# The order of ScalarE's work in slot 0 of a Mamba scan loop

## Chip, cores and metric

One core of one Trainium2 chip runs the whole kernel in float32. The metric is the device time of one launch in microseconds, the median of several runs. One core has five engines with separate instruction queues: TensorE (PE), VectorE (DVE), ScalarE (ACT), GpSimd (POOL) and SyncE (SP), which here issues the DMAs. In the profile PEld is TensorE's loading of weights.

## What is computed

The input x has 16 images of 96 channels and 64 x 64 pixels. Layer 0 is a graph convolution: a 1x1 convolution, then in each 8 x 8 window the 9 nearest of 64 nodes, an edge product with GELU, the maximum over the neighbours, another 1x1 convolution and a residual. Layer 1 runs two Mamba blocks over the 4096 pixels as a sequence, then a fusing 1x1 convolution, batch normalisation and a residual. The part of the reference that the change concerns:

```python
mu = seq.mean(-1, keepdims=True)
var = ((seq - mu) ** 2).mean(-1, keepdims=True)
h = (seq - mu) * jax.lax.rsqrt(var + EPS) * ln_g + ln_b
xz = h @ in_w
...
delta = jax.nn.softplus(dt @ dt_w + dt_b)
A = -jnp.exp(A_log)
dA = jnp.exp(delta[..., None] * A)
dBx = delta[..., None] * Bm[:, :, None, :] * xc[..., None]
...
hstates = jax.lax.associative_scan(comb, (dA, dBx), axis=1)[1]
y = jnp.einsum('blds,bls->bld', hstates, Cm) + Dp * xc
y = y * jax.nn.silu(z)
return y @ out_w
```

Here the model width is 96, the inner width 192, and there are 16 states.

## The kernel before

The sequence of each image is cut into 8 pieces of 512 pixels. An *item* is one piece in one of the two Mamba blocks of one image; there are 256 items, numbered n = 16 b + 8 i + k (image b, block i, piece k). The 16 states of an item are taken in pairs, so that an item has 8 *slots*, p = 0 to 7, and the main loop (L742 on) runs over 2048 slots. In a slot VectorE does three products `db` of `u` with `bt` (L646) and three scans (L788); ScalarE makes the three decays `da` that the scans read (L635); TensorE spreads one pair of rows of B over the partitions into `bt` (L641), one slot ahead; GpSimd multiplies the scanned states with C (L804); TensorE adds these up over the states (`folded`, L654 to L659), one slot behind. When the last fold of an item is done, in slot 0 of the next one, `gate` multiplies the sum with the gate z (L665, L666) in slot 1. VectorE, the product before the gate and the scans after it stand in one queue.

The instructions of each engine run in the order in which the program issues them. That order is written by hand: the rest of the work is held in Python generators, each of which issues one step per slot, after the slot's first scan. They stand in two lists:

- `preps`: the preparation of the item two ahead (`prelude`). It starts in slot 4. Its fifth step falls into slot 0 of the next item and is the softplus: Exp, +1, Ln, -1 on ScalarE (L595, L597, L599, L600). GpSimd takes it up in slot 1 (L602).
- `going`: `norm` of the item two ahead, whose first step in slot 0 is the product `pc` (L521) and its Square on ScalarE (L523), and whose second in slot 1 is `pvar` (L526), Ln and Exp (L528, L529); `tail`, which for an item of the second block has in slot 0 the fusing product `po` (L690) and its copy `o` on ScalarE (L692); `edges` and `nearest`, the graph convolution of later pieces. In slot 0 `edges` has the products `pv` (L386, L387) and their copy `vu` on ScalarE (L389). In slot 2 and 3 it has the products `t` and the GELUs (L406 to L414).

The products of these steps share a pool of two PSUM tiles, `pm`, tag "mm", in rotation: a product waits until the reader of the last but one is done. `bt` has one PSUM tile of its own.

The decays and the C rows (`ct`) of a slot are issued by `ahead`, two slots before they are used (`AHEAD = 2`). As a rule that is done at the end of a slot, unless a step in the slot has changed ScalarE's table of functions (it yields `TABLE`). In the slots of `FIRST` it is done ahead of the slot's steps. The lines in the slot:

```python
                open_steps()
                if p in FIRST:
                    ahead()
                held = False
                for several in (preps, going) if p == 0 else (going, preps):
                    for steps in list(several):
                        step = next(steps, several)
```

Of the kernel before, what the change touches and what calls it, by code (L numbers as in the profile page):

```python
# [20 lines left out]
def tile_conv_knn_mamba(ctx: ExitStack, tc: tile.TileContext, w: dict, out: bass.AP):  # L21
# [248 lines left out]
    def close_steps():  # L270
        while closing:
            products, use = closing.pop(0)
            opening.append(partial(use, products()))

    def open_steps():
        while opening:
            opening.pop(0)()
# [205 lines left out]
    def pooled(b):  # L483

        mean = pr.tile([C, 1], F32, tag="mean1", name=f"mean1_{b}")
        nc.vector.reduce_sum(mean, means.pop(b), AX.X)
        yield
        pg = pm.tile([C, 1], F32, tag="mm", name=f"pg_{b}")
        nc.tensor.matmul(pg, lhsT=gpT, rhs=mean, start=True, stop=True)
        yield  # L490
        gp = pr.tile([C, 1], F32, tag="gp", name=f"gp_{b}")
        nc.scalar.activation(gp, pg, AF.Relu, bias=gp_b[:, 0, :], scale=1.0 / L)
        yield
        gc = pr.tile([C, 1], F32, tag="gc", name=f"gc_{b}")

        def product():
            ps = pm.tile([C, 1], F32, tag="mm", name=f"pg2_{b}")
            nc.tensor.matmul(ps, lhsT=fusT[:, 1, :], rhs=gp, start=True, stop=True)
            return ps

        apart(product, lambda ps: nc.vector.tensor_tensor(gc, ps, fus_b[:, 0, :], ALU.add))
        yield
        gcs[b] = gc
# [6 lines left out]
    def norm(n):  # L510

        b, i, k = items[n]
        nm = f"{b}_{i}_{k}"
        seq = seqs[b, k]
        hn = hns[n % NHN]
        if k == 0:
            nc.gpsimd.memset(hn[:, :HALO], 0.0)
        else:
            nc.gpsimd.tensor_copy(hn[:, :HALO], hns[(n - 1) % NHN][:, Q:])
        pc = pm.tile([C, Q], F32, tag="mm", name=f"pc_{nm}")  # L520
        nc.tensor.matmul(pc, lhsT=cmat, rhs=seq, start=True, stop=True)  # L521
        sq = pr.tile([C, Q], F32, tag="sq", name=f"sqv_{nm}")
        nc.scalar.activation(sq, pc, AF.Square)  # L523
        yield
        ps = pm.tile([C, Q], F32, tag="mm", name=f"pvar_{nm}")
        nc.tensor.matmul(ps, lhsT=ones_cc, rhs=sq, start=True, stop=True)  # L526
        rs = pr.tile([C, Q], F32, tag="rs", name=f"rs_{nm}")
        nc.scalar.activation(rs, ps, AF.Ln, bias=eps_t[:C], scale=1.0 / C)  # L528
        nc.scalar.activation(rs, rs, AF.Exp, scale=-0.5)  # L529
        yield  # L530
        nc.gpsimd.tensor_tensor(hn[:C, HALO:], seq, rs, ALU.mult)  # L531
# [107 lines left out]
    def bcast(n, p):  # L639
        bt = pb.tile([128, Q], F32, tag="bt", name=f"bt_{n}_{p}")  # L640
        nc.tensor.matmul(bt, lhsT=bsel[:, p, :], rhs=made[n][2], start=True, stop=True)  # L641
        return bt

    def times_b(n, p, c, bt):
        db = pd.tile([128, Q], F32, tag="db", name=f"db_{n}_{p}_{c}")
        nc.vector.tensor_tensor(db, made[n][5][:, c, :], bt, ALU.mult)  # L646
        return db
# [15 lines left out]
    def gate(n, y):  # L663
        z = made[n][1]
        nc.vector.tensor_tensor(z[:, :Q], z[:, :Q], y[0], ALU.mult)  # L665
        nc.vector.tensor_tensor(z[:, Q:], z[:, Q:], y[1], ALU.mult)  # L666

    def tail(n):

        b, i, k = items[n]  # L670
        nm = f"{b}_{i}_{k}"
        seq = seqs[b, k]
        z = made[n][1]

        def product():
            po = pm.tile([C, Q], F32, tag="mm", name=f"pow_{nm}")
            nc.tensor.matmul(po, lhsT=out_w[i][:, 0, :], rhs=z[:, :Q], start=True, stop=False)
            for h in range(2):
                nc.tensor.matmul(
                    po[:, bass.ts(h, QH)], lhsT=out_w[i][:, 1 + h, :], rhs=z[:, Q:], start=False, stop=(h == 1)  # L680
                )
            return po

        apart(product, lambda po: nc.vector.tensor_tensor(seq, seq, po, ALU.add))  # L684
        del made[n]
        if i == NL - 1:
            yield
            yield
            po = pm.tile([C, Q], F32, tag="mm", name=f"po_{nm}")
            nc.tensor.matmul(po, lhsT=fusT[:, 0, :], rhs=seq, start=True, stop=True)  # L690
            o = pr.tile([C, Q], F32, tag="xn", name=f"o_{nm}", bufs=1)
            nc.scalar.activation(o, po, AF.Identity, bias=gcs[b])  # L692
            yield
            yield
            nc.vector.bn_stats(stats[:, b * NQ + k, :], o)
            nc.sync.dma_start(out=o_d[b][:, bass.ts(k, Q)], in_=o)
# [21 lines left out]
        drain(prelude(n))  # L718

    AHEAD = 2  # L720
    FIRST = (0, 2, 4)
    order = [(n, p) for n in range(NI) for p in range(NPR)]
    coming = deque(order)
    soon = {}
# [1 line left out]
    def ahead():  # L726
        if coming:
            t = coming.popleft()
            soon[t] = chosen(*t)
# [5 lines left out]
    going, preps = [edges(0, NQ - 2)], []  # L735
# [6 lines left out]
    for m, (n, p) in enumerate(order):  # L742
        b, i, k = items[n]
        nm = f"{b}_{i}_{k}"
        after = order[m + 1] if m + 1 < len(order) else None

        if n % 2 == 1 and p == 5 and near_row < NB * NQ:
            going.append(nearest(*divmod(near_row, NQ)))
            near_row += 1
        if n % 2 == 1 and p == 5 and edge_row < NB * NQ:  # L750
            going.append(edges(*divmod(edge_row, NQ)))
            edge_row += 1
        between.extend(later[0])
        later = [later[1], []]
        if p == 0 and k == 0:
            state = pr.tile([128, NPR, NB3], F32, tag="state", name=f"state_{nm}")
        if p == 0 and i == 0 and k == 5:
            going.append(pooled(b))
        if p == 0 and n + 2 < NI:
            going.insert(0, norm(n + 2))  # L760
        if p == 4 and n + 2 < NI:
            preps.append(prelude(n + 2))
        ct, das = soon.pop((n, p))
        dbs = [first, times_b(n, p, 1, bt), times_b(n, p, 2, bt)]
        if after is not None:
            bt = bcast(*after)
        hb = pr.tile([128, NB3, Q], F32, tag="hb", name=f"hb_{nm}_{p}", bufs=3)
        for c in range(NB3):
            if c == 1:
                if p == 1 and n:  # L770
                    gate(n - 1, y)
                if p == 6 and n:
                    going.append(tail(n - 1))
                open_steps()
                if p in FIRST:
                    ahead()
                held = False

                for several in (preps, going) if p == 0 else (going, preps):
                    for steps in list(several):  # L780
                        step = next(steps, several)
                        held = held or step is TABLE
                        if step is several:
                            several.remove(steps)
                close_steps()
            if c == 2 and after is not None:
                first = times_b(*after, 0, bt)
            nc.vector.tensor_tensor_scan(  # L788
                hb[:, c, :], das[c], dbs[c], state[:, p, c : c + 1] if k else 0.0, ALU.mult, ALU.add
            )  # L790
            if between and c < 2 and p not in (0, 1):
                between.popleft()()  # L792
            while c == 1 and late:
                late.pop(0)()
        if behind is not None:
            if p == 1:
                y = [
                    py.tile([128, Q], F32, tag="ya", name=f"ya_{nm}"),
                    py.tile([128, QH], F32, tag="yb", name=f"yb_{nm}"),
                ]  # L800
            folded(*behind, y)
        if k + 1 < NQ:
            nc.gpsimd.tensor_copy(state[:, p, :].unsqueeze(2), hb[:, :, Q - 1 : Q])  # L803
        nc.gpsimd.tensor_tensor(hb, hb, ct.unsqueeze(1).to_broadcast([128, NB3, Q]), ALU.mult)  # L804
        behind = (n, p, hb)
        while not held and len(soon) < AHEAD and coming:
            ahead()
# [53 lines left out]
```

## Time and profile before

| | |
|---|---|
| median of 3 runs | 13931.91 us (13919.25 to 13937.55) |
| the profiled execution: its time | 13931.85 us |
| the profiled execution: its span | 13930.0 us |
| mean granted TensorE clock | 0.953 of full speed |
| first scan starts | 401.86 us into the span |

A page of the profile lists for each group of instructions their line, engine, operation, tiles, count, busy time and mean length, then the idle time of the engine before them and what ended it. The scans and products dominate VectorE: 6144 products `db` of 685 ns and 6144 scans, most of them of 1276 ns. A wait is read as "engine, tile, line, waiting for engine, tile, line". Idle time of an engine matters only if it is the one that sets the end, or if it hands its lateness on to that one.

### The profile page before, as it was taken

Reading aid. Unit: us, or ns where it says so; the run is one execution under the profiler, and the core shown is the slowest. Engines: PE = TensorE matmul, PEld = TensorE weight load, DVE = VectorE, ACT = ScalarE, POOL = GpSimd, SP = SyncE. Lnnn points to the kernel's source line nnn. Section 1 sums busy time; section 2 is a strip of 40 time slices with the busy share of each in tenths; the row PEclk is TensorE's granted clock in tenths of the full one; section 3 lists DMA queues with packets and bytes.
Section 4 is the critical chain, followed back from the end, with each engine's and each line's share of the span. In section 5 each row is a group of like instructions: output and inputs, shape, how many; then the busy total and the mean of one; then the engine's idle time right before and its main releaser. Section 6 shows DMA issues by size and latency. Waiting matters only on the chain. (4 is left out here: it accounts for less than half of the span.)

```text
span 13930.0 us, 162083 instructions
## 1 busy us (share of the span) xinstructions
PE 12335.4 (89%) x47944; PEld 4659.8 (33%) x47944; DVE 12860.6 (92%) x16894; ACT 9963.9 (72%) x14645; POOL 10740.5 (77%) x6407
## 2 busy tenths in 40 slices
PE   5899999999999999999999999999999999999881
PEld 2333333333333333333333333333333333333320
DVE  2799999999999999999999999999999999999994
ACT  4677777777777777777777777777777777777652
POOL 1687878788787787878788787887878888787781
PEclk8999999999999999999999999999999999999995
DMA  1233333333333333333333333333333333333327
GB/s 27 74 83 88 87 80 88 85 82 87 85 84 86 85 85 83 85 84 83 87 85 84 85 87 82 84 87 84 84 87 86 81 87 86 81 85 88 81 81 230
DMA packets 887144, 1206.19 MB, mean 87 GB/s; under 512 B 282272, under 2 KB 413742, under 8 KB 877040
## 3 DMA queue, kind: packets, MB, share of 16 engines
q1 hardware_dynamic: 871792, 1169.34, 32.4%
q10 hardware_dynamic: 14464, 26.48, 0.5%
q8 instruction: 377, 6.18, 0.2%
q14 instruction: 511, 4.19, 0.1%
HBM read 706.82 MB, written 85.72 MB: 57 GB/s over the span
## 5 line engine op out<-in xcount | busy, mean ns | idle before, releaser
L804 POOL TENSOR_TENSOR hb<-hb,ct 128x1536 f32<-128x1536 f32 x2048 | 7067.0, 3451 | 599.9 <-issue 190.9
L788 DVE TENSOR_TENSOR_SCAN hb<-da,state,db 128x512 f32<-128x512 f32 x5376 | 6842.8, 1276 | 0.0
L646 DVE TENSOR_TENSOR db<-u,bt 128x512 f32<-128x512 f32 x6144 | 4009.7, 685 | 201.5 <-PE bt L641 198.4
L635 ACT ACTIVATE da<-delta,a 128x512 f32<-128x512 f32 x6144 | 3904.8, 716 | 30.1 <-DVE hb L788 19.4
L641 PE MATMUL bt<-dbl,bsel 128*128 128x512 f32 x4096 | 2359.8, 659 | 279.0 <-DVE db L646 269.5
L657 PE MATMUL ya<-hb,fold 128*64 128x512 f32 x8192 | 2273.9, 634 | 123.9 <-POOL hb L804 123.2
L803 POOL COPY state<-hb 128x3 f32<-128x3 f32 x1792 | 335.9, 187 | 1942.0 <-DVE hb L788 1846.2
L414 ACT ACTIVATE g<-t,eb,es 128x512 f32<-128x512 f32 x1536 | 1171.8, 776 | 899.2 <-PE t L406 655.3
L659 PE MATMUL yb<-hb,fold 128*64 128x256 f32 x8192 | 1284.4, 393 | 0.0
L659 PEld LDWEIGHTS yb<-hb,fold 128*64 128x64 f32 x8192 | 610.5, 142 | 1252.6 <-issue 1251.7
L641 PEld LDWEIGHTS bt<-dbl,bsel 128*128 128x128 f32 x4096 | 627.0, 193 | 1143.7 <-DVE db L646 632.3
L406 PE MATMUL t<-oh,vu 128*128 128x512 f32 x2048 | 985.6, 603 | 20.8 <-ACT g L414 20.8
L788 DVE TENSOR_TENSOR_SCAN hb<-da,db 128x512 f32<-128x512 f32 x768 | 926.6, 1213 | 16.1 <-ACT da L635 16.1
L548 PE MATMUL pj<-hn,conv_in 128*128 128x512 f32 x2048 | 929.2, 596 | 9.1 <-POOL hn L531 9.1
L560 ACT ACTIVATE xc<-pj,conv_b 128x512 f32<-128x512 f32 (+1 forms) x512 | 297.1, 580 | 797.8 <-PE pj L553 671.8
L657 PEld LDWEIGHTS ya<-hb,fold 128*64 128x64 f32 x8192 | 498.8, 140 | 1038.1 <-issue 610.2
L375 POOL TENSOR_SCALAR oh<-idb,node 64x1024 f32<-64x1024 uint16 x256 | 730.8, 2855 | 126.3 <-DMA idb<-idxd 126.3
L409 PE MATMUL t<-oh,vu 128*64 128x512 f32 x2048 | 553.3, 618 | 183.5 <-ACT g L414 180.4
L528 ACT ACTIVATE rs<-pvar,eps_t 96x512 f32<-96x512 f32 x256 | 174.7, 683 | 689.8 <-PE pvar L526 687.7
L792 DVE TENSOR_REDUCE hqa<-g 128x64 f32<-128x512 f32 x976 | 651.3, 667 | 0.0
L406 PEld LDWEIGHTS t<-oh,vu 128*128 128x128 f32 x2048 | 390.2, 193 | 528.8 <-issue 413.7
L548 PEld LDWEIGHTS pj<-hn,conv_in 128*128 128x128 f32 x2048 | 392.6, 192 | 510.5 <-issue 498.1
(166 smaller groups left out, 17319.8 us busy)
## 6 DMA issues: line engine op xcount, KB each, us to landing
ct<-cd SPq DMA_DIRECT2D x4096, 128.0 KB
delta<-ln SPq DMA_DIRECT2D x1024, 128.0 KB
u<-s SPq DMA_DIRECT2D x1024, 128.0 KB
idb<-idxd SPq DMA_DIRECT2D x256, 256.0 KB
delta<-ln SPq DMA_DIRECT2D x1024, 64.0 KB
u<-s SPq DMA_DIRECT2D x1024, 64.0 KB
x<-in_x SPq DMA_DIRECT2D x128, 192.0 KB
rn<-r4d SPq DMA_DIRECT2D x128, 192.0 KB
```

The lines of the kernel that those rows point to most:

```text
L375: nc.gpsimd.tensor_scalar(ohj, numbers, node, None, ALU.is_equal)
L406: nc.tensor.matmul(t, lhsT=vus[p][:, part, :128], rhs=ohw[part], start=True, stop=True)
L414: nc.scalar.activation(g, t, AF.Gelu, bias=e_b[:, j : j + 1], scale=e_s[:, j : j + 1])
L548: nc.tensor.matmul(ps, lhsT=wt[:, t, :128], rhs=hn[:, off : off + Q], start=(t == 0), stop=(t == taps - 1))
L635: nc.scalar.activation(da, delta[:, c, :], AF.Exp, scale=a_neg[i][:, c, p : p + 1])
L641: nc.tensor.matmul(bt, lhsT=bsel[:, p, :], rhs=made[n][2], start=True, stop=True)
L646: nc.vector.tensor_tensor(db, made[n][5][:, c, :], bt, ALU.mult)
L657: nc.tensor.matmul(y[0][half(h)], lhsT=fold, rhs=hb[:, h, :], start=False, stop=(p == NPR - 1))
L659: nc.tensor.matmul(y[1][half(h)], lhsT=fold, rhs=hb[:, 2, bass.ts(h, QH)], start=False, stop=(p == NPR - 1))
L788: nc.vector.tensor_tensor_scan(hb[:, c, :], das[c], dbs[c], state[:, p, c : c + 1] if k else 0.0, ALU.mult, ALU.add)
L792: between.popleft()()
L804: nc.gpsimd.tensor_tensor(hb, hb, ct.unsqueeze(1).to_broadcast([128, NB3, Q]), ALU.mult)
```

## The change

Two edits, both in the main loop:

```diff
     AHEAD = 2
-    FIRST = (0, 2, 4)
+    FIRST = (2, 4)
...
                 held = False
-
-                for several in (preps, going) if p == 0 else (going, preps):
+                for several in (going, preps):
```

With the first, the decays and C rows of slot 2, which slot 0 issued before its steps, are issued at its end, as in slots 1, 3, 5, 6 and 7. With the second, the softplus in slot 0 is issued after the steps of `going` and not before them. In slot 0 ScalarE has then: the Square, `vu`, `o` where there is one, the four softplus passes, the three decays. Before it had: the three decays, the four softplus passes, the Square, `vu`, `o`. No instruction is added or removed.

## The prediction

> **What bounds the kernel now.** First the page's busy times (engine, busy us, share of the span, instructions):
>
> ```profile
> PE 12335.4 (89%) x47944; PEld 4659.8 (33%) x47944; DVE 12860.6 (92%) x16894; ACT 9963.9 (72%) x14645; POOL 10740.5 (77%) x6407
> ```
>
> VectorE is the bound; it stands still for 1069 us of the 13930.0 us span. About half of that lies before the first slot, in the first two items or in the closing normalisation, which the change doesn't touch. So next the waits of DVE alone (total us, times, longest us):
>
> ```profile
> DVE z L665 <- PE ya L657: 359.9, 121, 5.0
> DVE db L646 <- PE bt L641: 198.4, 202, 48.0
> ```
>
> The gate of the previous item (L665) waits for its last fold on TensorE in 121 of 256 items. That is the largest stall inside the loop. Some 57 us of the second row fall at the start; about 140 us are short waits in slots 2 and 3. Why the fold is late is read from the timeline of one item (start us, length us, instruction, count, idle before it and its releaser):
>
> ```profile
> 7010.36 3.79 ACT L635 ACTIVATE da<-delta,a 128x512 f32<-128x512 f32 x6
> ...
> 7011.68 1.02 PE L521 MATMUL pc<-x,cmat 96*96 96x512 f32 x2
> ...
> 7017.55 0.57 ACT L523 ACTIVATE sqv<-pc 96x512 f32<-96x512 f32 x1
> ...
> 7018.18 2.02 PE L690 MATMUL po<-x,fusT 96*96 96x512 f32 x2 [4.67 <-ACT sqv L523]
> ...
> 7022.15 0.69 DVE L665 TENSOR_TENSOR z<-z,ya 128x512 f32<-128x512 f32 x1 [4.54 <-PE ya L657]
> ```
>
> The reader is to see the chain: pc is ready at 7012.70, but its square starts at 7017.55, since ScalarE has six decays and four softplus passes (7014.03 to 7017.65) ahead of it. The product L690 needs the PSUM buffer that the square frees, so it waits 4.67 us, and the fold (7020.13, behind it on PE) lets the gate go only at 7022.15. The fold's operand was ready at 7013.87, when L804 ended.
>
> Two more lines of the same kind name what gets worse. Who waits for the logarithm L528 (total us, times):
>
> ```profile
>   PEld pv L386: 94.2, 120
> ```
>
> 120 is the number of even items with edges: there slot 1 takes one PSUM tile more (L308), so pv comes back to the buffer that L528 reads. In item 148, even and without L690, this reads:
>
> ```profile
> 8111.88 0.68 ACT L528 ACTIVATE rs<-pvar,eps_t 96x512 f32<-96x512 f32 x1 [2.00 <-PE pvar L526]
> ...
> 8116.35 1.13 PE L641 MATMUL bt<-dbl,bsel 128*128 128x512 f32 x2
> ...
> 8118.31 0.67 DVE L646 TENSOR_TENSOR db<-u,bt 128x512 f32<-128x512 f32 x1
> ```
>
> bt ends at 8117.48 and DVE wants it at 8118.31: 0.83 us of slack between L528 and a DVE stall.
>
> **What the Trainium skill says.** *PSUM — Partial Sum Buffer*, section "Engine vs sequencer instructions": ScalarE's queue is strictly first in, first out, and matmuls start and complete in program order. The chain above is just that: one waiting square holds ScalarE's work behind it, one waiting product holds the fold. *TensorE: Matmul & The Clock Gate*, "What's actually happening": the array falls to half rate after an idle window of about 3.4 us, and the windows run free. The trace agrees: L690 takes 2.02 us above and 1.10 us in item 138, where PE waited less; and a less idle PE is cut too, in item 153:
>
> ```profile
> 8357.60:8361.10 3.50, 1.27 (x3) 0.44 (x4) 3.47 (x9) 3.35 (x6) 3.40 (x2) 1.00 0.17 60
> 8361.10:8364.50 3.40, 3.40 (x11) 1.13 (x12) 3.40 (x5) 1.55 (x4) 2.31 (x4) 0.50 0.24 77
> ```
>
> (stretch; its length and PE's busy us; PEld, DVE, ACT, POOL; granted clock, DMA.) With 1.27 us of 3.50 busy the next stretch gets clock 0.50. *ScalarE: Activation LUTs*, "What ACT_TABLE_LOAD costs": a load takes about 1283 ns and consecutive ACTIVATEs overlap by about 93 ns. The trace shows 1283 ns, and the loads stand at L414, L451, L560 and L567 only, in slots 2 to 5; the moved instructions already run side by side without one, so the change adds none.
>
> **The change part by part.** Nothing is added or removed; in slot 0 ScalarE's order goes from [da for slot 2 x3, softplus x4, square, vu, (o)] to [square, vu, (o), softplus x4, da x3]. PE's and POOL's order stays: neither moved step issues there. On SP the two ct loads of slot 2 go behind the slot's other DMAs (in even items the x1 store, which waits for L475); their reader, L804 of slot 2, comes some 15 us later, so this costs nothing. The decays are wanted at slot 2's first scan.
>
> I walk ScalarE through slot 0 with the trace's durations: three decays 1.98, softplus 3.62, square 0.57, vu 0.46, o 0.68, and sort the items by parity and by whether L690 stands in slot 0 (n mod 16 in 10 to 15, 0, 1; about 60 of each kind that matter).
>
> *Odd with L690* (the item above): decays of slot 1 end at 7012.34; square 7012.74 to 7013.31; vu to 7014.0; L690 follows pv directly, 7013.5 to 7014.6 at full rate; fold to 7016.2. DVE comes to the gate at 7017.6: no wait. o ends at 7015.4, softplus at 7018.9, the decays at 7020.8, before a second slot that starts at about 7023. Length of slot 1 from first scan to first scan: 11.60 us now, 6.69 in odd items without L690. Gain 60 x 4.9 = 294 us.
>
> *Odd without L690*: no gate wait now. But the square is late here too; pvar (L526) waits 1.4 us for it, PE's idle time adds up and the clock halves (item 153), and bt comes 2.26 us late. With the square early that idle time goes. Waits in slots 2 and 3 of n mod 16 = 3, 7, 9: 12.6 + 7.1 + 21.7 = 41 us; lost overlap 2; and I take 10 of the 21 us in items 5, where pooling adds its own wait. Gain 53 us.
>
> *Even without L690* (item 148): pc ends only at 8106.70, behind pf2, fold and bt on PE, while ScalarE has done slot 1's decays by 8103.7. It used to fill those 3 us with the decays and softplus that now stand behind. Square to 8107.31, vu 8107.54 to 8108.00, softplus to 8111.53, decays to 8113.41, L528 at 8113.32 instead of 8111.88: 1.44 later. pv and bt follow it on PE: bt ready at 8118.95, wanted at 8118.31: 0.65 us stall in slot 2. The table load and gelus of slot 2 are 1.44 late too; next bt ready 8124.8, wanted 8123.61 + 0.65: 0.53. By slot 4 there was 1.6 us of slack, so it ends there. With 0.08 of lost overlap per wait, 1.34 us, 61 items: loss 82 us. Bounds: 0 (if PE finds room) to 2.7 (if its clock halves as well).
>
> *Even with L690*: now 2.24 us of waits per item in some four pieces, 2.6 with the overlap. The gate's wait goes, but o also stands ahead of softplus: in item 138 L528 comes at 7586.1, bt at 7591.8 against a wish at 7590.4: 1.36, then 0.45. PE is idle 2.6 us before pv, so the clock will mostly halve, about 1.2 more. After: 2.9; loss 0.3 x 60, say 20 us; bounds -1 to +1.5 per item.
>
> Sum: -294 - 53 + 82 + 20 = -245. From the profiled execution's own 13931.85 us (the median of the runs is 13931.91, the same) this gives about 13687 us.
>
> **Rivals.**
> 1. *As worked out*, the stall of odd items goes and even items pay a little: 13687, own range 13630 to 13760. Chance 0.58.
> 2. *Even items don't pay*: L528's lateness is absorbed. -294 - 53 and up to -100 from the even items with L690: 13931.85 - 347 - 50 = 13535, or up to 13585 with little from those. For: POOL and DVE have no other wait there. Against: pv's 120 waits on L528 show that this edge is already live. 0.12.
> 3. *Even items pay double*, PE idle before pv halving the clock in both kinds: 61 x 2.7 = 165 and 60 x 1 = 60; 13931.85 - 347 + 225 = 13810. 0.19.
> 4. *The fold stays late* for another reason, say o or POOL's L804, so the stall keeps its size: 13930. Against: L804 is done at 7013.87. 0.04.
> 5. *Slower*: pv behind L528 becomes the new gate wait. ScalarE idles in slot 0 of even items until pc, everything behind slides, L528 comes 3 or more us late instead of 1.44, PE idles, runs at half clock, and bt is late in slots 2, 3 and 4. It decides from 347/121 = 2.9 us more per even item; at 4 us the time is 13931.85 - 347 + 484 = 14069. For: both halves of the mechanism are in the trace. Against: ScalarE's walk leaves 2 us less than that. 0.07.
>
> Differences under 0.2% (28 us) can't be told from no change here. Faster: 1, 2, 3 and a little of the rest, 0.89; same 0.04; slower 0.07. The range that holds 8 in 10 takes case 1, most of 3 and the near end of 2: 13580 to 13830.
>
> **What would show it.** Right: L665's wait on L657 falls below 40 us; L690 no longer waits for L523 and takes near 1.1 us; slot 1 of odd items is 6.7 us in all. The even items' cost: pv's wait on L528 grows from 94 to some 250 us and DVE's wait for bt stays near 200 us though the odd items' part is gone. Wrong: DVE waiting for da (L635) in slot 2, which would mean that the decays are late; waits for bt above 400 us, which would mean case 5; L665 still waiting, case 4.

## The result and the profile after

The changed kernel takes 13704.78 us (median of 4 runs, 13695.32 to 13709.56), the kernel before 13925.98 us in the runs beside it (13919.25 to 13937.55). The ratio is 0.9839, with a 95% interval of 0.9822 to 0.9857: 221 us faster. The forecast was 13687 us, in a range of 13580 to 13830.

The profiled execution's span fell from 13930.0 to 13693.4 us. Its busy times, and two lines of DVE's waits (total us, times, longest us):

```profile
PE 12153.1 (89%) x47944; PEld 4619.7 (34%) x47944; DVE 12849.1 (94%) x16894; ACT 9998.7 (73%) x14645; POOL 10747.1 (78%) x6407
```

```profile
DVE db L646 <- PE bt L641: 352.7, 314, 46.4
...
DVE z L665 <- PE ya L657: 5.7, 1, 5.7
```

The work is the same; DVE's busy time is 12 us less of 12860, so the other 225 of the 237 us are idle time that is gone. The gate (L665) waited 359.9 us and now waits 5.7, once, at the very end of the loop. In its place the wait for `bt` rose from 198.4 to 352.7 us. (One line is gone from the file, so L787 and L803 are the old L788 and L804.)

The timeline of item 127, whose stall the prediction showed, now reads (start us, length us, instruction, idle before it):

```profile
6890.44 0.59 ACT L523 ACTIVATE sqv<-pc 96x512 f32<-96x512 f32 x1 [0.43 <-PE pc L521]
...
6891.13 1.10 PE L690 MATMUL po<-x,fusT 96*96 96x512 f32 x2
...
6892.16 1.08 PE L657 MATMUL ya<-hb,fold 128*64 128x512 f32 x4
...
6892.91 0.83 ACT L595 ACTIVATE e<-e 128x768 f32<-128x768 f32 x1
...
6895.22 0.67 DVE L665 TENSOR_TENSOR z<-z,ya 128x512 f32<-128x512 f32 x1
...
6910.88 0.70 DVE L646 TENSOR_TENSOR db<-u,bt 128x512 f32<-128x512 f32 x1 [0.91 <-PE bt L641]
```

The square starts 0.04 us after `pc`, the product L690 follows at full rate, and the fold ends 2 us before DVE comes to the gate. The last line, from slot 3, is new: DVE waits 0.91 us for `bt`, where this item had no such wait before. It is taken up with `ahead_even` below.

Item 138 (even, with L690) shows the larger new wait:

```profile
7444.06 1.96 ACT L635 ACTIVATE da<-delta,a 128x512 f32<-128x512 f32 x3
...
7449.06 0.59 ACT L523 ACTIVATE sqv<-pc 96x512 f32<-96x512 f32 x1 [3.04 <-PE pc L521]
...
7456.81 0.67 ACT L528 ACTIVATE rs<-pvar,eps_t 96x512 f32<-96x512 f32 x1
...
7458.34 1.68 PE L654 MATMUL ya<-xc,dp_diag 128*128 128x512 f32 x2
7459.81 1.06 PE L655 MATMUL yb<-xc,dp_diag 128*128 128x256 f32 x2
7460.80 1.75 PE L657 MATMUL ya<-hb,fold 128*64 128x512 f32 x4
...
7464.07 0.70 DVE L646 TENSOR_TENSOR db<-u,bt 128x512 f32<-128x512 f32 x1 [2.78 <-PE bt L641]
```

ScalarE stands idle for 3.04 us until `pc` is there, and does the softplus and the decays after that, so L528 comes late. `pv` waits for the buffer that L528 reads. L654, L655 and L657, behind `pv` on PE, took 1.12, 0.59 and 1.08 us elsewhere and here take 1.68, 1.06 and 1.75. So `bt` is 2.78 us late for DVE. Those who wait for L528 in the changed kernel, in all (total us, times):

```profile
  PEld pv L386: 332.3, 120
  PE pv L386: 229.8, 120
```

To see which items gained and lost, I added up, in each trace, the distances from the first scan of an item to the first scan of the next, by the four kinds of the prediction (n from 2 to 243; the head gives the number of items), and took the difference to the kernel before (us):

| run | even without L690, 61 | odd without L690, 61 | even with L690, 60 | odd with L690, 60 | median of the run |
|---|---|---|---|---|---|
| predicted | +82 | -53 | +20 | -294 | 13687 |
| changed kernel | +80.8 | -54.5 | +11.0 | -261.8 | 13704.78 |
| order_only | +1.2 | -67.2 | -147.4 | -286.7 | 13421.12 |
| decays_only | +0.6 | -62.1 | -153.7 | -154.5 | 13555.91 |
| decays_between | +80.5 | -57.6 | +12.4 | -265.7 | 13707.64 |
| ss_later | +75.9 | -57.5 | -35.5 | -268.5 | 13649.50 |
| ahead_even | +0.7 | -49.7 | -147.5 | -245.9 | 13484.54 |
| ahead_odd | +83.7 | -65.6 | +38.6 | -294.3 | 13683.88 |
| pe_kept_busy | +88.1 | -54.9 | -39.8 | -279.2 | 13633.92 |
| even_t_twice | +2.2 | -44.4 | -147.4 | -296.7 | 13446.14 |
| order_t_twice | +2.2 | -56.1 | -147.5 | -294.6 | 13433.79 |

### The profile page after: what moved, and what is told of

Same layout as the page of the kernel before. It is cut to its first block, busy times and chain, and to the rows that moved or that the text cites. A ratio compares the mean times of both kernels' runs of the same rounds, so it can differ in the third digit from the quotient of the medians.

```text
span 13693.4 us, 162089 instructions
## 1 busy us (share of the span) xinstructions
PE 12153.1 (89%) x47944; PEld 4619.7 (34%) x47944; DVE 12849.1 (94%) x16894; ACT 9998.7 (73%) x14645; POOL 10747.1 (78%) x6407
## 5 line engine op out<-in xcount | busy, mean ns | idle before, releaser
L803 POOL TENSOR_TENSOR hb<-hb,ct 128x1536 f32<-128x1536 f32 x2048 | 7068.4, 3451 | 524.2 <-PE yb L659 65.9
L787 DVE TENSOR_TENSOR_SCAN hb<-da,state,db 128x512 f32<-128x512 f32 x5376 | 6811.0, 1270 | 0.0
L646 DVE TENSOR_TENSOR db<-u,bt 128x512 f32<-128x512 f32 x6144 | 3986.3, 679 | 352.7 <-PE bt L641 352.7
L641 PE MATMUL bt<-dbl,bsel 128*128 128x512 f32 x4096 | 2325.3, 650 | 444.3 <-DVE db L646 430.6
L657 PE MATMUL ya<-hb,fold 128*64 128x512 f32 x8192 | 2221.6, 621 | 85.2 <-POOL hb L803 84.5
L659 PE MATMUL yb<-hb,fold 128*64 128x256 f32 x8192 | 1252.9, 385 | 0.0
L787 DVE TENSOR_TENSOR_SCAN hb<-da,db 128x512 f32<-128x512 f32 x768 | 924.2, 1209 | 17.0 <-ACT da L635 17.0
L657 PEld LDWEIGHTS ya<-hb,fold 128*64 128x64 f32 x8192 | 495.2, 138 | 956.5 <-issue 487.0
L409 PE MATMUL t<-oh,vu 128*64 128x512 f32 x2048 | 560.9, 626 | 227.5 <-ACT g L414 224.2
L386 PE MATMUL pv<-ewT,y 96*64 96x192 f32 x2048 | 467.0, 354 | 230.1 <-ACT rs L528 229.8
```

The source lines that it names most:

```text
L657: nc.tensor.matmul(y[0][half(h)], lhsT=fold, rhs=hb[:, h, :], start=False, stop=(p == NPR - 1))
L659: nc.tensor.matmul(y[1][half(h)], lhsT=fold, rhs=hb[:, 2, bass.ts(h, QH)], start=False, stop=(p == NPR - 1))
L787: nc.vector.tensor_tensor_scan(hb[:, c, :], das[c], dbs[c], state[:, p, c : c + 1] if k else 0.0, ALU.mult, ALU.add)
```

## The experiments

The kernel before took 13928 to 13934 us beside all of them. The ratios are to it. The traces also record which clock TensorE was granted at each moment; "half rate" or "half clock" below means a granted clock of 0.5 of full speed.

**The two edits apart.** `order_only` is the kernel before with the second edit alone:

```diff
-                for several in (preps, going) if p == 0 else (going, preps):
+                for several in (going, preps):
```

> Only the softplus goes behind the copies and squares; the decays of slot 2 stay ahead of slot 0's steps. Theory (even items pay in the changed kernel because ScalarE idles 3 us until pc and the decays and softplus then stand behind): in even items the decays fill that idle time, softplus ends about 9.8 us into the window of item 148 instead of the decays at 11.7, L528 starts at 10.2 again, and pv's wait on L528 falls back below 100 us. In odd items the square comes at 7014.7 instead of 7013.3 in the old item's clock, still before the gate is due. So all gains and no loss: 13931.85 - 294 (odd with L690) - 53 (odd without) - 156 (even with L690) = about 13430 us, DVE's wait for bt below 120 us. Rival (the decays ahead of the steps are part of what held the square up, both edits are needed): L665 waits again 1 to 2 us in odd items, 13750 to 13850 us.

Measured: 13421.12 us, ratio 0.9632 (0.9616 to 0.9648). `decays_only` has the first edit alone:

```diff
-    FIRST = (0, 2, 4)
+    FIRST = (2, 4)
```

> Only the decays of slot 2 go to the end of slot 0; the softplus stays ahead of the copies and squares. Theory: in even items softplus (3.6 us) fills the time until pc, so L528 is not late and there is no new wait; in odd items the square ends at 7016.3 in the old item's clock instead of 7013.3, L690 ends at 7017.5 to 7018.4 (PE idles 2.9 us, part of it at half clock), and the gate waits 0.8 to 2.5 us instead of 4.5. Sum: -53 (odd without L690) - 156 (even with) - 190 (odd with) = about 13530 us; L665's wait 60 to 150 us in total. Rival (only the order of softplus and square matters): 13850 to 13930 us, L665's wait over 250 us.

Measured: 13555.91 us, ratio 0.9729 (0.9712 to 0.9745). Both came out near the expected 13430 and 13530 us. So each edit alone is better than both together. What the whole change costs in even items is there in neither: +1.2 and +0.6 where it has +80.8, and about -150 where it has +11. In item 138 of `order_only`:

```profile
7301.36 3.79 ACT L635 ACTIVATE da<-delta,a 128x512 f32<-128x512 f32 x6
...
7306.36 0.59 ACT L523 ACTIVATE sqv<-pc 96x512 f32<-96x512 f32 x1 [1.21 <-PE pc L521]
...
7312.28 0.67 ACT L528 ACTIVATE rs<-pvar,eps_t 96x512 f32<-96x512 f32 x1
...
7318.52 0.67 DVE L646 TENSOR_TENSOR db<-u,bt 128x512 f32<-128x512 f32 x1
```

Six decays instead of three fill the time until `pc`; ScalarE idles 1.21 us and not 3.04. L528 comes 10.92 us after the first decay, where it took 12.75, and DVE doesn't wait for `bt`. (`pv` still waits 136.4 us on PEld for L528 in all, not the less than 100 that I expected; DVE has slack for that.) In `decays_only` softplus does the filling, but in odd items it stands before the square:

```profile
DVE z L665 <- PE ya L657: 128.0, 61, 5.0
```

This is inside the 60 to 150 us that were expected, 2.1 us each time. The rival theories of both runs fell.

**Which of the two is last doesn't matter.** `decays_between` is the changed kernel with the decays ahead of the softplus, both behind the rest:

```diff
                 for several in (going, preps):
+                    if p == 0 and several is preps:
+                        ahead()
```

> In slot 0: copies and squares, then the decays of slot 2, then the softplus. Theory (what costs time in even items is ScalarE's idle stretch ahead of pc, with 5.6 us of work behind it and before L528, not which of the two kinds of work is last): the same time as the changed kernel, 13705 us within 20. Rival (the decays come too late for slot 2, and that costs the time): 50 to 130 us faster, 13575 to 13655 us.

Measured: 13707.64 us, ratio 0.9839 (0.9822 to 0.9855), and nearly the same sums by kind. In both kernels DVE waits for `da` twice in all, at the very start (17.0 and 17.5 us). So the lateness of the decays for their own reader is not what costs. What is left is the work that stands before L528, which the next run takes up.

**The buffer.** `ss_later` is the changed kernel with L308 one slot later, so that `pv` of even items no longer takes the buffer of `pvar`:

```diff
         nc.gpsimd.tensor_tensor(sq, y, y, ALU.mult)
         yield
+        yield
         ss = pm.tile([C, Q], F32, tag="mm", name=f"ss_{nm}")
...
         nc.sync.dma_start(out=r4[:, 1], in_=ss_d.rearrange("o (p j) -> (o p) j", j=QJ))
         yield
-        yield
```

> The changed kernel, with the product ss (L308) of the neighbour search one slot later, in slot 2, so that pv in slot 1 of even items takes the PSUM buffer of pc or o and not the one that L528 reads. Theory (PE's wait of pv on L528 is what makes bt late in slot 2): that wait goes (332 us on PE to about 0), bt is in time in slot 2, and of the 308 us of DVE's waits for bt inside the loop those in slot 3 remain and grow a little, since table load and GELU are still late: 13705 - 110 = about 13595 us. Rival (bt is late for another reason, the fold waiting for POOL or PE's own work): no change, 13705 us within 20.

Measured: 13649.50 us, ratio 0.9798 (0.9782 to 0.9815), 55 us faster than the changed kernel and not 110. The wait of `pv` for L528 is gone whole, and with it DVE's wait in slot 2 of even items. But in slot 3 it is 1.04 us in item 148 and 1.65 in item 138, more than the 0.43 of item 148 in the changed kernel. Its timeline (lines below L313 have numbers one lower):

```profile
7945.85 1.02 PE L308 MATMUL ss<-sq,ones_cc 96*96 96x512 f32 x2
...
7947.94 1.28 ACT L413 ACT_TABLE_LOAD   x1
...
7950.07 1.08 PE L408 MATMUL t<-oh,vu 128*64 128x512 f32 x4 [0.96 <-ACT g L413]
...
7952.37 1.13 PE L640 MATMUL bt<-dbl,bsel 128*128 128x512 f32 x2
...
7953.53 0.70 DVE L645 TENSOR_TENSOR db<-u,bt 128x512 f32<-128x512 f32 x1 [1.04 <-PE bt L640]
```

ScalarE's lateness comes through by a second way: the table load and the GELU are late, L408 waits for the GELU, and `bt` of the next slot stands behind L408. The edit itself puts `ss` and its copy into slot 2, ahead of the table load, but that is not why the load is late: in even items without L690 it starts 3.28 us after the slot's first scan both here and in the changed kernel (mean of 61), and after 1.87 us in `order_only`. So the buffer carries the stall of slot 2. Taking it away brings back 46 us in the even items with L690, of the 158 between the changed kernel and `order_only`; part of that is the clock, for only 6 of these 60 items have a stretch at half rate, where the changed kernel has 48. In the other even items it only moves the stall.

**The clock.** `pe_kept_busy` is the changed kernel; in even items with L690, PE makes `ss` three times into the same tile while it would wait for L528:

```diff
-        nc.tensor.matmul(ss, lhsT=ones_cc, rhs=sq, start=True, stop=True)
+        for _ in range(3 if now[0] >= 2 and items[now[0] - 2][1] else 1):
+            nc.tensor.matmul(ss, lhsT=ones_cc, rhs=sq, start=True, stop=True)
```

(`now[0]` is the number of the current item.)

> The changed kernel; in even items with L690 the product ss is made three times into the same tile, so that PE works on where it otherwise waits 2.5 us for L528. Theory (of the 2.8 us that DVE waits for bt in slot 2 of these items, the half clock after PE's idle stretch makes some 1.5): the wait falls to about 1.15 where it was 2.8 to 3.3, and 0.43 comes in slot 3: 60 us faster than the changed kernel, about 13645 us, though PE has 120 products more. Rival (the clock makes no difference to bt): no change or slower, 13705 us or more.

Measured: 13633.92 us, ratio 0.9786 (0.9772 to 0.9799): 71 us faster than the changed kernel, 51 of it in the even items with L690, although PE makes 120 products more. In item 138 (the line numbers are one to two higher here):

```profile
7423.24 2.74 PE L309 MATMUL ss<-sq,ones_cc 96*96 96x512 f32 x6
...
7427.53 1.13 PE L655 MATMUL ya<-xc,dp_diag 128*128 128x512 f32 x2
...
7431.62 0.70 DVE L647 TENSOR_TENSOR db<-u,bt 128x512 f32<-128x512 f32 x1 [1.13 <-PE bt L642]
```

The diagonal product is back at 1.13 us and the wait at 1.13 instead of 2.78. The granted clock over these stretches, first of the changed kernel, then of `pe_kept_busy` (columns as in the prediction; 0.85 and 0.65 are means of full and half rate):

```profile
7456.40:7459.80 3.40, 2.26 (x10) 1.12 (x11) 3.40 (x5) 3.37 (x7) 3.05 (x3) 0.85 0.00 1
7459.80:7463.20 3.40, 3.40 (x12) 1.31 (x11) 1.49 (x2) 3.38 (x6) 3.40 (x3) 0.65 0.34 96
```

```profile
7426.80:7430.20 3.40, 3.40 (x20) 1.58 (x20) 3.40 (x5) 3.40 (x7) 3.40 (x2) 1.00 0.02 1
```

In `pe_kept_busy` none of the 60 items has a stretch at half rate, in the changed kernel 48 have one. So of the 2.78 us in this item 1.65 go back to PE's half clock after its pause before `pv`, and 1.13 are L528's own lateness. But 0.43 us of the 1.65 come back as a wait in slot 3, so that the clock costs 1.22 us net.

**Even and odd items apart.** `ahead_even` takes the decays ahead in even items alone, `ahead_odd` in odd items alone; the softplus order is the changed one in both:

```diff
-                if p in FIRST:
+                if p in FIRST or (p == 0 and n % 2 == 0):
```

> The changed kernel, but in even items the decays of slot 2 are taken ahead of slot 0's steps again; odd items as in the changed kernel. Theory (the loss sits in even items alone, since only there pc is late and pv needs L528): it goes whole, as with the order of softplus changed alone, which took 13421 us; the 12 us that the gate still waited there go too: 13405 to 13425 us. Rival (odd items lose as well by their late decays): 13480 to 13600 us.

> The changed kernel, but in odd items the decays of slot 2 are taken ahead of slot 0's steps; even items as in the changed kernel. Theory: even items keep their loss and odd items gain nothing: 13705 to 13720 us. Rival (late decays cost in all items): 13500 to 13600 us.

Measured: 13484.54 us, ratio 0.9677 (0.9664 to 0.9690), and 13683.88 us, ratio 0.9822 (0.9807 to 0.9837). Here my theory missed a part, and both runs lie outside the ranges that it gave; `ahead_odd` lies outside its rival's range too. Even items behave as expected: the loss goes whole when they take the decays ahead. But odd items are dearer as well by their late decays, 41 and 18 us in `ahead_even` against `order_only`, together 58 of the 63 us between the two medians; and they gain 33 and 11 us in `ahead_odd` against the changed kernel. (There the even items with L690 lose 28 us more than in the changed kernel; 55 of them have a stretch at half rate, where the changed kernel has 48, and PE runs at half rate for 239 us in them instead of 164. Why, is not shown.) The rival's span of 13480 to 13600 us is where `ahead_even` landed. The timelines of item 139 show where, first `ahead_even`, then `order_only`:

```profile
7393.31 1.13 PE L641 MATMUL bt<-dbl,bsel 128*128 128x512 f32 x2 [0.98 <-DVE db L646]
...
7398.18 1.60 PE L409 MATMUL t<-oh,vu 128*64 128x512 f32 x4 [2.02 <-ACT g L414]
...
7399.56 1.92 PE L657 MATMUL ya<-hb,fold 128*64 128x512 f32 x4
...
7403.34 0.70 DVE L646 TENSOR_TENSOR db<-u,bt 128x512 f32<-128x512 f32 x1 [0.91 <-PE bt L641]
```

```profile
7364.77 1.12 PE L641 MATMUL bt<-dbl,bsel 128*128 128x512 f32 x2 [0.33 <-DVE db L646]
...
7369.02 1.08 PE L409 MATMUL t<-oh,vu 128*64 128x512 f32 x4 [1.41 <-ACT g L414]
...
7373.79 0.68 DVE L646 TENSOR_TENSOR db<-u,bt 128x512 f32<-128x512 f32 x1
```

In the first the table load and the GELU are 0.6 us later, so L409 waits 2.02 instead of 1.41 us; then L409 and the fold take 1.60 and 1.92 us instead of about 1.08, and `bt` is 0.91 us late. Whether that is the clock after a longer pause, or the lateness of the GELU in itself, the last two runs were to tell. They make one product `t` twice in slot 2 of odd items, in the time in which PE would wait for L409:

```diff
-                        nc.tensor.matmul(t, lhsT=vus[p][:, part, :128], rhs=ohw[part], start=True, stop=True)
+                        for _ in range(2 if (hf, p, part) == (1, 0, 1) else 1):
+                            nc.tensor.matmul(t, lhsT=vus[p][:, part, :128], rhs=ohw[part], start=True, stop=True)
```

> As the run with the decays ahead in even items (13484.5 us), but in slot 2 of odd items the second product t (L406) is made twice into the same tile, so that PE has 0.9 us less to wait for the GELU before L409. Theory (what odd items still lose to late decays, 58 us against the run with the order of softplus changed alone, is PE's half clock after a wait of 2.0 us in place of 1.4): the wait falls to some 1.1 us, PE stays at full rate, bt is in time in slots 3 and 4: 13420 to 13440 us. Rival (bt is late because table load and GELU are late): no gain, 13480 to 13500 us.

> The run with the order of softplus changed alone (13421 us), with the same product t made twice. Theory: PE doesn't fall to half clock at that place here, so the added product, made in PE's waiting time, changes nothing: 13421 us within 15. Rival (a busier PE is faster in itself): 13400 us or less.

Measured: 13446.14 us, ratio 0.9654 (0.9641 to 0.9668), and 13433.79 us, ratio 0.9646 (0.9633 to 0.9659). The added product takes 38 us off `ahead_even` (6 us above the expected range, 34 below the rival's) and puts 13 us on `order_only`. In odd items with L690 the loss goes whole (-245.9 to -296.7). So the clock is the cause there, and the other runs bear it out. This is how many of the 60 odd items with L690 have a stretch at half rate that begins in slot 2, beside their sum from the table:

| run | items at half rate in slot 2 | sum, us |
|---|---|---|
| ahead_even | 39 | -245.9 |
| changed kernel | 27 | -261.8 |
| decays_between | 24 | -265.7 |
| ss_later | 21 | -268.5 |
| pe_kept_busy | 13 | -279.2 |
| ahead_odd, even_t_twice, order_t_twice | 0 | -294.3 to -296.7 |

Each such item costs about 1.2 us. (`order_only` has none in slot 2, but 11 that begin in slot 0, where the gate still waits; its sum is -286.7.) That also accounts for the 17 us by which `pe_kept_busy` beats the changed kernel in odd items with L690, which it doesn't edit.

In odd items without L690, 23 us remain against `order_only`, or 12 against its own control: there the added product itself makes the items with pooling (n mod 16 = 5) slower. Of the 12 us, 11 are in those 15 items. It isn't the clock, for `even_t_twice` has no stretch at half rate in any odd item; the table load is still 0.75 us later than in its control (means over the kind), and DVE waits 21.2 us for `bt` in slot 3 where it waits 10.0 in the control. That fits the rival of `even_t_twice`, a table load and GELU that are late in themselves; no run separates it further.

`order_only` is the best of all: 13421 us, 284 us below the changed kernel, by undoing one of its two edits. In its trace DVE is 96% busy.

## Why the prediction was right

*The stall of the odd items with L690.* Right in mechanism, sign and place: slot 1 fell to 6.69 us, and L690 no longer waits for the square on PE. The term was given as -294 us and measured -261.8. What was left out, and so put at nothing, is the wait for `bt` in slots 3 and 4 that `ahead_even` isolates. L528, and the table load and GELU behind it, stand behind the decays and are late in odd items too, by 0.6 us in item 139. That is enough to lengthen PE's pause before L409 so far that the clock halves in 27 of the 60. The prediction followed PE's idle time in even items, but here it ended the walk at the gate, with "no wait". Where no such stretch occurs, in `ahead_odd`, the sum is -294.3: the gain itself was sized right.

*Odd items without L690*: -53 predicted, -54.5 measured. That the early square keeps PE's clock up and so removes the 2.26 us waits of slot 2 held: before, 29 of these items had a stretch at half rate that began in slot 1, and in the changed kernel none has. The figure owes something to luck. With the decays left ahead, in `order_only`, the same items gain 67.2; late decays cost about 13 us, 9 of them in the items with pooling, where the prediction had cautiously taken only 10 of 21 us.

*Even items without L690*: +82 predicted, +80.8 measured. The walk gave L528 1.44 us later and stalls of 0.65 and 0.53; item 148 of the changed kernel has 0.51 and 0.43 in the timeline. Several items of this kind (n mod 16 = 8, and one now and then of the others) wait longer, which brings the sum up to the forecast. So the close agreement is in part luck. That the stall has the two ways that the prediction gave it, the buffer in slot 2 and the table load with the GELU in slot 3, is what `ss_later` shows.

*Even items with L690*: +20 predicted, +11.0 measured. The gate's wait is gone, and in item 138 2.78 us for `bt` stand in its place. The prediction walked to 1.36 and 0.45 us without the clock, and took about 1.2 for the clock. `pe_kept_busy`, without half rate, has 1.26 and 0.48 on average, and the clock's net cost in item 138 is 1.22: each term came out close.

*The counterweights as a whole.* The prediction named what L528 would hold up, and `pv`'s wait on it grew to 332.3 us on PEld; the text said some 250. Its sign that DVE's wait for `bt` would stay near 200 us failed: it is 352.7. That sign went against the prediction's own walk, whose waits in even items, 61 x 1.18 and 60 x 3.0 us, come to about 250 (measured: 231) besides some 57 at the start. The 24 us by which the sum was off (221 instead of 245) are about the 32 us missing in odd items with L690, less the 9 that the even items with L690 did better.

One reading of the prediction is not right for its item 127: there no square waits and holds ScalarE's work up; the square itself stands behind ten passes. A square that waits is what the changed kernel has in even items, 3.04 us in item 138.

What the prediction did not draw is the conclusion that the two edits work against each other: its own sentence, that ScalarE "used to fill those 3 us", says that one of the two kinds of work should stay ahead. Its case 2, in which even items don't pay, was put at 13535 us; `order_only`, which takes the cause of that payment away, took 13421.

## What to carry over

On an engine that isn't the bound, ask two questions of every instruction that is moved: who waits for what it now precedes, and what fills the time that it used to fill. Work that nobody waits for yet belongs into the engine's idle stretches, here before `pc` on ScalarE; moved behind, it turns the idle stretch into lateness for everything that follows. And when two edits serve the same end, measure each alone: here either alone gave more than both.

## What was not expected of the hardware

The sentence of the Trainium skill that the prediction cites (*TensorE: Matmul & The Clock Gate*, "What's actually happening") ties half rate to an idle window of about 3.4 us. In these traces shorter pauses bring it on, in stretches where PE is partly busy. In item 139 of `ahead_even`:

```profile
7395.20:7398.60 3.40, 1.38 (x5) 0.33 (x5) 3.40 (x5) 3.37 (x5) 3.40 (x3) 1.00 0.00 0
7398.60:7402.00 3.40, 3.40 (x12) 0.96 (x8) 3.37 (x7) 0.97 (x2) 3.32 (x3) 0.50 0.01 2
```

PE is busy for 1.38 of 3.40 us, and half rate follows. Nor does the length of the pause decide alone. Before L409 PE paused for 2.0 to 2.1 us in all 60 odd items with L690 of `ahead_even`; 39 fell to half rate and 21 did not. With pauses of 1.1 to 1.7 us in `order_only` none of the 60 did. Of the 76 stretches at half rate in that trace, 50 last 3.41 us and 12 last 6.83, twice that, which fits windows of one length. That these windows run free, as the prediction quotes, would explain why the same pause costs one item and not the next; no run here tests it.

So in item 139 0.6 us of lateness on ScalarE became 0.91 us on DVE, where the 1.41 us pause of `order_only` had cost nothing. A redundant product in a wait was then worth its cost: `pe_kept_busy` gained 71 us of 13705 with 120 products made for nothing. The same trick where the clock was not at stake (`order_t_twice`) cost 13 us.
